# A two-layer recurrent and attention kernel on one core: loads of the first chunk on one queue, its copies on VectorE, B prepared early, and the norms of layer 0 in one ordered list

## The chip, the cores and the metric

The kernel runs on one core of a Trainium2 chip. The engines of the core are named as the profile names them: PE (TensorE, matrix products; PEld is its weight load), DVE (VectorE), ACT (ScalarE), POOL (GpSimd) and SP (SyncE, which here only issues loads and stores). Each works through its own queue in order and they meet at semaphores. The metric is device time in microseconds (us); the median of three runs is used, and one further execution is profiled. All times below are us unless another unit stands there.

## The reference

Input x is 16 sequences of 256 tokens of 256 numbers, f32, so 4096 tokens. Two layers follow, each of the form x + s * silu(g), with s and g computed from the same layer norm of x. Layer 0 has a complex diagonal recurrence for s and a GELU network for g; layer 1 has latent attention with 16 heads for s and a base matrix with a two-expert low-rank addition for g. Cut to layer 0, which the change touches:

```python
xn = _layernorm(x, axis=-1)
# s: recurrence with 32 complex states
A_re, A_im = mag * cos(theta), mag * sin(theta)     # mag = exp(-exp(softplus(nu_log)))
gamma = sqrt(clip(1.0 - mag * mag, 0.0))
Bu_re, Bu_im = xn @ (gamma * B_re).T, xn @ (gamma * B_im).T
new_re = A_re * h_re - A_im * h_im + bu_re          # scanned over the 256 tokens
new_im = A_re * h_im + A_im * h_re + bu_im
s = H_re @ C_re.T - H_im @ C_im.T + D * xn
# g: feed-forward
h = gelu(xn @ proj1.T + proj1_bias)                 # 256 -> 1024
g = silu(h @ proj2.T + proj2_bias)                  # 1024 -> 256
x = x + s * g
xn = _layernorm(x, axis=-1)                         # then layer 1 in the same form
```

## The kernel before, in words

The 4096 tokens are cut into 8 chunks of 512 tokens (two sequences each). A chunk lies in SBUF as four tiles of 128 tokens by 256 numbers and stays there through both layers. Layer 0 goes over all chunks, then layer 1 over all chunks; layer 1's code is not touched.

For a chunk of layer 0 these names matter:

- `layer_norm`, called by `norm0(ch)`: on DVE, statistics of four tiles (`bn_stats`, `bn_aggr`) and `ve` = variance + eps; on POOL a power, `rs`; on DVE again four subtract-and-multiply instructions that give `xn`.
- `turn0(ch, xn)`: PE transposes the eight 128 x 128 blocks of xn into PSUM (`tp`), and one copy by ACT and one by DVE give `xnT`.
- `hidden(ch, xnT)`: PE makes `ph` from `p1T` and xnT, ACT applies GELU, giving `hT`, eight blocks.
- `recur(ch, xnT)`: PE makes `pb` from `bT` (B, scaled and transposed) and xnT. DVE multiplies it by `turn`, a table of angles, giving `v`; two transfers over SP swap its halves into `w`; POOL adds; DVE scans with `decay` and multiplies again, giving `g`.
- `fold_heads(g)`, for chunks 0 to 3: small products (`psq`, `pso`) that fold weights of layer 1.
- `mix(ch, jp, hT)`: PE makes `pf` from hT and `p2T` for half a chunk; DVE adds a bias and ACT applies SiLU, giving `zf`.
- `finish0`: PE makes `py` from g and `csc` (C, signed); POOL and DVE put the new x together (`dx`).

The tables come from the two columns of `par`: exponents computed by polynomial (`exp_of`), `mag`, `gam`, the gain `gs`, the angle's sine and cosine (`sh`, `chf` on ACT), doublings of angle (`rot`), then `turn`, `decay`, `bsc` (B scaled) and `csc`. These are about 200 instructions on a few columns, most of them 0.15 to 0.25 on DVE.

What sets the order: instructions that are free are placed by a scheduler when the program is built, by its own estimate of when things are ready. Where a function calls an `InOrder` object instead of an engine, each instruction gets a dependency on the last one of that object, so their order on that engine is the written one. All of PE's work goes through one such object, `pe`. In layer 0 there are also `v0` for DVE, `a0` for ACT and `g0` for POOL. `Later` holds the small instructions of the tables back in a list and writes them out by count, so that they can be laid between other work. `start()` writes out chunk 0 by hand: two half chunks, with norm, transposes and hidden products, and table work between them.

Before the change, `v0` holds the work of `start()`, the table work and the norms of chunks 1 to 3. The norms of chunks 4 to 7, the products `v`, the copy of `bT`, and the powers in `layer_norm` are free for the scheduler. In the main loop the written order of a chunk from 2 on is: hidden, recur, (fold_heads), norm0 and turn0 of the next chunk, mix of the first half, finish0, mix of the second half, finish0. The same loop for chunks 0 and 1 is written a little differently, with the turn of B (`turn_b`) after the hidden products of chunk 1.

The loads: SP issues the four tiles of chunk 0 first (line 109), then half of p2T, the other chunks and layer 1's weights. ACT issues both halves of p1T (lines 224 and 225), the bias, signs, B, C, half of p2T and two broadcast rows (up to line 234). POOL issues par. All instructions that go through an `InOrder` object carry line 52 in the profile.

Of the kernel before, what the change touches and what calls it, by code (L numbers as in the profile page):

```python
# [11 lines left out]
F32 = mybir.dt.float32  # L12
I32 = mybir.dt.int32
AF = mybir.ActivationFunctionType
ALU = mybir.AluOpType
# [3 lines left out]
P = 128  # L19
B, S, D = 16, 256, 256  # L20
NTOK = B * S
CH = 512
NCH = NTOK // CH
TPC = CH // P
NST = 32
FF = 1024
# [14 lines left out]
def tile_two_layers(ctx: ExitStack, tc: tile.TileContext, d: dict, out: bass.AP):  # L41
    nc = tc.nc
# [23 lines left out]
    class Later:  # L66


        def __init__(self):
            self.todo = []  # L70

        def on(self, engine):
            later = self
# [7 lines left out]
            return Engine()  # L81

        def write(self, n=None):
            n = len(self.todo) if n is None else n
            for f in self.todo[:n]:
                f()
            del self.todo[:n]

    pe = InOrder(nc.tensor)

# [7 lines left out]
    X = []  # L98
# [1 line left out]
        xt = xpool.tile([P, TPC, D], F32, tag=f"x{ch}", name=f"x{ch}")  # L100
        X.append(xt)

    def load_x(ch):
        nc.sync.dma_start(
            X[ch], x_dram[ch * CH : (ch + 1) * CH, :].rearrange("(j p) e -> p j e", p=P)
        )

    for j in range(TPC):
        nc.sync.dma_start(X[0][:, j, :], x_dram[j * P : (j + 1) * P, :])

    ident = const.tile([P, P], F32, tag="ident", name="ident")
    make_identity(nc, ident)
# [46 lines left out]
        nc.sync.dma_start(desc, d["desc"])  # L159


    def layer_norm(pool, src, dst, tag, v=nc.vector):
        st = pool.tile([P, TPC, 6], F32, tag="ln_st", name=f"st_{tag}")
        mv = pool.tile([P, TPC, 2], F32, tag="ln_mv", name=f"mv_{tag}")
        ve = pool.tile([P, TPC], F32, tag="ln_ve", name=f"ve_{tag}")
        rs = pool.tile([P, TPC], F32, tag="ln_rs", name=f"rs_{tag}")
        for j in range(TPC):
            v.bn_stats(st[:, j, :], src[:, j, :])
        for j in range(TPC):
            v.bn_aggr(mv[:, j, :], st[:, j, :])  # L170
        v.tensor_scalar(ve, mv[:, :, 1], LN_EPS, None, ALU.add)
        nc.gpsimd.tensor_tensor(rs, ve, mhalf, ALU.pow)
        for j in range(TPC):
            v.tensor_scalar(
                dst[:, j, :], src[:, j, :], mv[:, j, 0:1], rs[:, j : j + 1],
                ALU.subtract, ALU.mult,
            )

    def transpose_rows(psum, ptag, src, dst, tag):
        for c in range(2):  # L180
            ps = psum.tile([P, CH], F32, tag=ptag, name=f"tp_{tag}_{c}")
            for j in range(TPC):
                pe.transpose(
                    ps[:, j * P : (j + 1) * P], src[:, j, c * P : (c + 1) * P], ident
                )
            if c == 0:
                nc.scalar.copy(dst[:, c, :], ps)
            else:
                nc.vector.tensor_copy(dst[:, c, :], ps)

    def bc(ap, n):

        return ap.unsqueeze(1).to_broadcast([ap.shape[0], n, ap.shape[1]])
# [6 lines left out]
    with ExitStack() as l0:  # L200
# [19 lines left out]

        p1d = d["proj1T"].rearrange("(c p) f -> p c f", p=P)
        p2d = d["proj2T"].rearrange("(c p) f -> p c f", p=P)
        nc.gpsimd.dma_start(par, d["par"])
        nc.scalar.dma_start(p1T[:, 0, :], p1d[:, 0, :])
        nc.scalar.dma_start(p1T[:, 1, :], p1d[:, 1, :])
        nc.scalar.dma_start(b1, d["proj1_b"])
        nc.scalar.dma_start(sgn, d["signs"])
        nc.scalar.dma_start(bst, d["B_stack"])
        for r in range(2):
            nc.scalar.dma_start(cst[64 * r : 64 * r + 64, :], d["C_stack"][r, 64 * r : 64 * r + 64, :])  # L230
        for z in range(2):
            (nc.sync, nc.scalar)[z].dma_start(p2T[:, 4 * z : 4 * z + 4, :], p2d[:, 4 * z : 4 * z + 4, :])
        nc.scalar.dma_start(b2_bc, d["proj2_b"].partition_broadcast(P))
        nc.scalar.dma_start(d_bc, d["D"].partition_broadcast(P))
        for ch in range(1, NCH):
            load_x(ch)
        load_layer1(wraw)

        def norm0(ch):
            xn = a2.tile([P, TPC, D], F32, tag="xn", name=f"xn0_{ch}")  # L240
            layer_norm(sm, X[ch], xn, f"0_{ch}", v0 if ch < 4 else nc.vector)
            return xn

        def turn0(ch, xn):
            xnT = a2.tile([P, 2, CH], F32, tag="xnT", name=f"xnT0_{ch}")
            transpose_rows(ps_mm, "mm", xn, xnT, f"0_{ch}")
            return xnT


        v0 = InOrder(nc.vector)  # L250
        a0 = InOrder(nc.scalar)
        later = Later()
        g0 = InOrder(nc.gpsimd)
        pv, pa, pg = later.on(v0), later.on(a0), later.on(g0)
# [30 lines left out]
        arg = tiny("arg")  # L285
        pv.tensor_scalar(arg, ex[:, 0:1], 1.0, -1.0, ALU.add, ALU.mult)
        mag = exp_of(arg, 1, "b")
        gam = tiny("gam")
        pv.tensor_tensor(gam, mag, mag, ALU.mult)
        pv.tensor_scalar(gam, gam, -1.0, 1.0, ALU.mult, ALU.add)  # L290
        pv.tensor_scalar(gam, gam, 0.0, None, ALU.max)
        gsq = tiny("gsq")
        pg.tensor_tensor(gsq, gam, phalf, ALU.pow)
        gs = tiny("gs")
        pv.tensor_tensor(gs, gsq, sgn[:, 0:1], ALU.mult)


        th = ex[:, 1:2]
        k2 = tiny("k2")
# [12 lines left out]
        pv.tensor_scalar(rr, rr, 3.2, -3.2, ALU.min, ALU.max)  # L312
        pv.tensor_scalar(ab, rr, -1.0, None, ALU.mult)
        pv.tensor_tensor(ab, ab, rr, ALU.max)
        pa.activation(sh, rr, AF.Sin, scale=0.5)
        pa.activation(chf, ab, AF.Sin, bias=halfpi, scale=-0.5)

        rot = w0.tile([P, 8, 2], F32, tag="rot", name="rot")
        u = tiny("u")
        f = tiny("f")  # L320
# [41 lines left out]
        pv.tensor_scalar(decay, decay, mag, None, ALU.mult)  # L362
        pv.memset(decay[:, :, 0:1], 0.0)

        bT = w0.tile([P, 2, P], F32, tag="bT", name="bT")
        bsc = w0.tile([P, D], F32, tag="bsc", name="bsc")
        pv.tensor_scalar(bsc, bst, gs, None, ALU.mult)

        def turn_b():
            psb = ps_mm.tile([P, 2, P], F32, tag="mm", name="psb")  # L370
            for c in range(2):
                pe.transpose(psb[:, c, :], bsc[:, c * P : (c + 1) * P], ident)
            nc.vector.tensor_copy(bT, psb)


        csc = w0.tile([P, D], F32, tag="csc", name="csc")
# [55 lines left out]
        def recur(ch, xnT):  # L432

            pb = ps_mm.tile([P, 2, S], F32, tag="mm", name=f"pb_{ch}")
            for c in range(2):
                pe.matmul(
                    pb.rearrange("p b s -> p (b s)"), bT[:, c, :], xnT[:, c, :],
                    start=(c == 0), stop=(c == 1),
                )
            v = a2.tile([P, 2, S], F32, tag="v", name=f"v_{ch}")  # L440
            nc.vector.tensor_tensor(v, pb, bc(turn, 2), ALU.mult)
# [39 lines left out]
        def start():  # L481
# [18 lines left out]
            def apply(js):  # L500
                for j in js:
                    v0.tensor_scalar(
                        xn[:, j, :], X0[:, j, :], mv[:, j, 0:1], rs[:, j : j + 1],
                        ALU.subtract, ALU.mult,
                    )
                z = slice(js[0] * P, (js[1] + 1) * P)
                ps = ps_mm.tile([P, 2, 2 * P], F32, tag="mm", name=f"tp_0_0_{js[0]}")
                for c in range(2):
                    for j2, j in enumerate(js):
                        pe.transpose(  # L510
                            ps[:, c, j2 * P : (j2 + 1) * P], xn[:, j, c * P : (c + 1) * P], ident
                        )
                a0.copy(xnT[:, :, z], ps)

            def hide(js, f0, f1):
                z = slice(js[0] * P, (js[1] + 1) * P)
# [7 lines left out]
                    a0.activation(hT[fc][:, z], ph, AF.Gelu, bias=b1[:, fc : fc + 1])  # L524

            stats((0, 1))
            later.write(7)
            apply((0, 1))
            stats((2, 3))
            later.write(8)  # L530
            hide((0, 1), 0, 4)
            apply((2, 3))
            hide((0, 1), 4, NFC)
            hide((2, 3), 0, NFC)
            later.write(30)
            xn2 = norm0(1)
            later.write()
            return xn, xnT, hT, xn2

        xn, xnT, hT, xn2 = start()  # L540
# [637 lines left out]
```

## Time and profile before

| what | us |
|---|---|
| median of three runs (973.28 to 975.37) | 975.35 |
| profiled execution | 976.5 |
| its span, first to last instruction | 974.7 |
| PE busy, 0 to 31 | 17.61 of 31 |
| PE busy, 31 to 64 | 28.84 of 33 |
| PE busy, 64 to 80 (granted clock 0.60) | 15.65 of 16 |
| PE busy, 80 to 184 | 104.00 of 104 |
| PE busy, 184 to 310 | 123.59 of 126 |
| PE busy, 310 to 930 | 614.22 of 620 |
| PE busy, 930 to 975 | 37.84 of 45 |

The lower part of the table is a cut of the span into stages: layer 0 ends a little before 300, and layer 1 fills the rest. The granted clock is the share of full speed that PE's throttle allowed; its mean over the span is 0.989. A PE that is busy at a granted clock of 0.5 takes about twice as long for the same products: chunk 0's `psq`, at 67.89, takes 3.51, and chunk 2's, at 113.39, takes 1.89. The busy share of the other engines is an average over stages with different limits and says nothing of what a change in one stage is worth. A row of the timeline gives start, duration, engine, line and operation, then output and inputs; neighbouring instructions of one kind are merged (x4), and a bracket at the end tells how long the engine had been idle and who released it.

### The profile page before, as it was taken

The page shows a single profiled execution, that of the slowest core. Times are in us where ns is not written, and L with a number is a line of the kernel's source. Part 1 is how long each engine was busy: PE and PEld are TensorE (multiplying, and loading weights), DVE is VectorE, ACT ScalarE, POOL GpSimd, SP SyncE. Part 2 cuts the span into 40 slices and gives each one's busy share as a digit, 9 for nine tenths or more (in the row PEclk, how much of TensorE's full clock was granted, in tenths as well). Part 3 has the DMA queues.
Part 4 walks back from the last instruction along what each step waited for, and adds up shares of the span by engine and source line. Part 5 has one row for each costly group of instructions (what it writes and reads, how often), then busy time and mean ns, then how long its engine had stood idle before and what let it go on. Part 6 is the DMA issues. An engine that isn't in the chain of part 4 may idle for free.

```text
span 974.7 us, 15632 instructions
## 1 busy us (share of the span) xinstructions
PE 941.8 (97%) x4730; PEld 678.9 (70%) x4730; DVE 597.2 (61%) x1880; ACT 429.0 (44%) x1422; POOL 421.0 (43%) x743
## 2 busy tenths in 40 slices
PE   4989999999999989999999999999999999999988
PEld 3848567666765656777777767777777777777776
DVE  5664414211215868967886796786688678677662
ACT  2321332233223545654564554555455455446540
POOL 3024333123313553554465445465545535536440
PEclk9979999999999999999999999999999999999999
DMA  9503000000001377787676778667767767777770
GB/s 307 179 14 116 12 1 11 11 11 1 11 12 23 93 191 202 192 214 177 182 194 197 170 179 211 168 178 202 193 162 190 213 173 185 192 182 189 219 198 28
DMA packets 197299, 136.04 MB, mean 140 GB/s; under 512 B 142432, under 2 KB 186848, under 8 KB 197216
## 3 DMA queue, kind: packets, MB, share of 16 engines
q1 hardware_dynamic: 194144, 129.27, 50.8%
q0 software_dynamic: 1376, 3.67, 1.0%
q10 hardware_dynamic: 1696, 2.10, 0.7%
q8 instruction: 38, 0.62, 0.3%
q14 instruction: 45, 0.37, 0.1%
HBM read 63.18 MB, written 52.95 MB: 119 GB/s over the span
## 4 chain that ended last, share of the span: by engine, by line
PE 87%; DVE 6%; DMA 2%; POOL 2%; issue 1%; SPq 1%; ACT 1%; ACTq 0%; POOLq 0%; DVEq 0%
PE pq L52 21%; PE sc L52 14%; PE po L52 10%; PE ph L52 10%; PE pf L52 9%; PE av L52 9%; PE pg L52 4%; PE pb L52 2%; PE pm L52 2%; PE py L52 1%; PE tp L52 1%; PE pkv L52 1%; PE psq L52 1%; SPq L52 1%; DMA x<-in_x_dram 1%
## 5 line engine op out<-in xcount | busy, mean ns | idle before, releaser
L52 ACT ACTIVATE pr<-sc,nm 128x256 f32<-128x256 f32 (+7 forms) x512 | 190.0, 381 | 285.8 <-DVE sr L52 193.6
L52 POOL TENSOR_SCALAR pr<-pr,sr 128x256 f32<-128x256 f32 (+7 forms) x512 | 192.3, 395 | 276.1 <-DVE sr L52 274.8
L52 PEld LDWEIGHTS sc<-kT,qg 128*128 128x128 f32 x1024 | 160.2, 191 | 63.4 <-issue 39.0
L52 PE MATMUL sc<-kT,qg 128*128 128x256 f32 (+7 forms) x1024 | 177.1, 307 | 5.6 <-DMA qg<-qrot 4.1
L52 DVE STREAM_TRANSPOSE turned<-pr 128x512 f32<-128x512 f32 x186 | 123.4, 688 | 14.8 <-POOL pr L52 14.0
L52 DVE TENSOR_REDUCE nm<-sc 128x1 f32<-128x256 f32 (+7 forms) x512 | 127.7, 301 | 6.6
L52 PE MATMUL pq<-xnT,wlat 128*128 128x512 f32 x256 | 123.7, 607 | 0.0
L52 PE MATMUL pq<-xnT,wrope 128*128 128x512 f32 x256 | 120.1, 593 | 0.0
L52 PE MATMUL ph<-xnT,p1T 128*128 128x512 f32 (+1 forms) x288 | 113.6, 554 | 4.4 <-ACT xnT L52 4.4
L52 PE MATMUL po<-wout,attT 128*128 128x256 f32 x512 | 115.8, 380 | 0.0
L52 PE MATMUL pf<-p2T,hT 128*128 128x256 f32 x512 | 113.1, 379 | 0.0
L52 PEld LDWEIGHTS po<-wout,attT 128*128 128x128 f32 x512 | 96.4, 190 | 20.9 <-issue 6.4
L52 PEld LDWEIGHTS pf<-p2T,hT 128*128 128x128 f32 x512 | 96.7, 190 | 13.7 <-issue 0.9
L52 ACT ACTIVATION_READ_ACCUMULATOR pr<-sc,nm 128x1 f32 x512 | 103.5, 202 | 0.0
L52 PEld LDWEIGHTS ph<-xnT,p1T 128*128 128x128 f32 x288 | 56.0, 195 | 57.6 <-issue 49.5
L52 PE MATMUL av<-pT,row 128*64 128x256 f32 (+1 forms) x1024 | 90.5, 329 | 0.2 <-DMA pT<-far 0.2
L52 POOL TENSOR_TENSOR qrot<-qmul,qmul 128x512 f32<-128x512 f32 x64 | 83.0, 1317 | 14.2 <-DVE sc L52 9.8
L52 DVE TENSOR_TENSOR qmul<-pq,rot_q 128x512 f32<-128x512 f32 x128 | 80.9, 675 | 0.0
L52 PEld LDWEIGHTS av<-pT,row 128*64 128x64 f32 x1024 | 64.2, 137 | 22.9 <-issue 0.5
L52 ACT ACTIVATE qg<-pq 64x512 f32<-64x512 f32 x128 | 75.5, 590 | 6.1 <-PE pq L52 5.4
L52 DVE TENSOR_TENSOR sc<-sc,kmask 128x96 f32<-128x96 f32 (+1 forms) x192 | 46.1, 240 | 50.2 <-PE sc L52 48.9
L52 PEld LDWEIGHTS pq<-xnT,wlat 128*128 128x128 f32 x256 | 46.2, 193 | 32.2 <-issue 32.1
(164 smaller groups left out, 912.7 us busy)
## 6 DMA issues: line engine op xcount, KB each, us to landing
far<-turned SPq DMA_DIRECT2D x248, 192.0 KB, 3.7
pT<-far SPq DMA_DIRECT2D x62, 768.0 KB, 4.8
qg<-qrot SPq DMA_DIRECT2D x256, 64.0 KB, 2.3
x<-in_x_dram SPq DMA_DIRECT2D x7, 512.0 KB, 8.9
out_dram<-o POOLq DMA_DIRECT2D x28, 128.0 KB, 3.4
wqn<-in_wq_nopeT_dram SPq DMA_DIRECT2D x4, 512.0 KB, 4.9
wo<-in_Wo_dram SPq DMA_DIRECT2D x4, 512.0 KB, 5.8
w<-v SPq DMA_DIRECT2D x16, 128.0 KB, 2.3
```

Of the source, the lines that this page charges most:

```text
L52: r = getattr(self.engine, name)(*args, **kw)
```

## The change

It has four parts.

1. Loads of chunk 0. All of them but four go to SP, in a written order: the four x tiles, the second half of p1T (now cut by columns of the hidden layer), B, chunk 1, p2T, two broadcast rows, C. ACT issues par, the first half of p1T, the bias and the signs.
2. Copies. In `start()`, the copies of the transposes of chunk 0 go from ACT to DVE, in v0's order; chunk 1's go through a0 and v0. The table work is laid out anew: marks in the `Later` list replace counts, the angle comes before the gain, and chunk 1's transposes move into `start()`.
3. B. `bsc` is computed at the end of the gain, not after the tables; its turn on PE moves between the two mixes of chunk 0, and its copy moves from DVE to ACT in a0's order.
4. Norms. `norm0` uses v0 and g0 for every chunk, and `v` in `recur` goes through v0 as well.

```diff
-    for j in range(TPC):
-        nc.sync.dma_start(X[0][:, j, :], x_dram[j * P : (j + 1) * P, :])
...
-    def layer_norm(pool, src, dst, tag, v=nc.vector):
+    def layer_norm(pool, src, dst, tag, v=nc.vector, g=nc.gpsimd, between=None):
...
-        nc.gpsimd.tensor_tensor(rs, ve, mhalf, ALU.pow)
+        g.tensor_tensor(rs, ve, mhalf, ALU.pow)
+        if between:
+            between()
...
-        nc.gpsimd.dma_start(par, d["par"])
-        nc.scalar.dma_start(p1T[:, 0, :], p1d[:, 0, :])
-        nc.scalar.dma_start(p1T[:, 1, :], p1d[:, 1, :])
-        nc.scalar.dma_start(b1, d["proj1_b"])
-        nc.scalar.dma_start(sgn, d["signs"])
-        nc.scalar.dma_start(bst, d["B_stack"])
+        s0 = InOrder(nc.sync)
+        a0 = InOrder(nc.scalar)
+        a0.dma_start(par, d["par"])
+        for j in range(TPC):
+            s0.dma_start(X[0][:, j, :], x_dram[j * P : (j + 1) * P, :])
+        for z, e in ((0, a0), (1, s0)):
+            fz = slice(z * FF // 2, (z + 1) * FF // 2)
+            e.dma_start(p1T[:, :, fz], p1d[:, :, fz])
+        a0.dma_start(b1, d["proj1_b"])
+        a0.dma_start(sgn, d["signs"])
+        s0.dma_start(bst, d["B_stack"])
+        load_x(1, s0)
+        for z in range(2):
+            s0.dma_start(p2T[:, 4 * z : 4 * z + 4, :], p2d[:, 4 * z : 4 * z + 4, :])
+        s0.dma_start(b2_bc, d["proj2_b"].partition_broadcast(P))
+        s0.dma_start(d_bc, d["D"].partition_broadcast(P))
         for r in range(2):
-            nc.scalar.dma_start(cst[64 * r : 64 * r + 64, :], d["C_stack"][r, 64 * r : 64 * r + 64, :])
-        for z in range(2):
-            (nc.sync, nc.scalar)[z].dma_start(p2T[:, 4 * z : 4 * z + 4, :], p2d[:, 4 * z : 4 * z + 4, :])
-        nc.scalar.dma_start(b2_bc, d["proj2_b"].partition_broadcast(P))
-        nc.scalar.dma_start(d_bc, d["D"].partition_broadcast(P))
-        for ch in range(1, NCH):
+            s0.dma_start(cst[64 * r : 64 * r + 64, :], d["C_stack"][r, 64 * r : 64 * r + 64, :])
+        for ch in range(2, NCH):
             load_x(ch)
...
-        def norm0(ch):
+        def norm0(ch, between=None):
             xn = a2.tile([P, TPC, D], F32, tag="xn", name=f"xn0_{ch}")
-            layer_norm(sm, X[ch], xn, f"0_{ch}", v0 if ch < 4 else nc.vector)
+            layer_norm(sm, X[ch], xn, f"0_{ch}", v0, g0, between)
...
-            transpose_rows(ps_mm, "mm", xn, xnT, f"0_{ch}")
+            if ch == 1:
+                transpose_rows(ps_mm, "mm", xn, xnT, f"0_{ch}", a0, v0)
+            else:
+                transpose_rows(ps_mm, "mm", xn, xnT, f"0_{ch}")
...
-            nc.vector.tensor_copy(bT, psb)
+            a0.copy(bT, psb)
...
-            nc.vector.tensor_tensor(v, pb, bc(turn, 2), ALU.mult)
+            v0.tensor_tensor(v, pb, bc(turn, 2), ALU.mult)
...
-                a0.copy(xnT[:, :, z], ps)
+                return ps
+
+            def keep(js, ps):
+                v0.tensor_copy(xnT[:, :, js[0] * P : (js[1] + 1) * P], ps)
...
             stats((0, 1))
-            later.write(7)
+            later.write(4)
             apply((0, 1))
+            ps = turn((0, 1))
             stats((2, 3))
-            later.write(8)
+            keep((0, 1), ps)
+            later.write(3)
+            apply((2, 3))
             hide((0, 1), 0, 4)
-            apply((2, 3))
+            ps = turn((2, 3))
+            later.write("exp")
+            keep((2, 3), ps)
             hide((0, 1), 4, NFC)
             hide((2, 3), 0, NFC)
-            later.write(30)
-            xn2 = norm0(1)
+            xn2 = norm0(1, lambda: later.write("angle"))
+            later.write("gain")
+            xnT2 = turn0(1, xn2)
             later.write()
...
             if ch == 0:
 
-                xnT2 = turn0(1, xn2)
-                zf = [mix(ch, jp, hT) for jp in range(2)]
+                zf = [mix(ch, 0, hT)]
+                turn_b()
+                zf.append(mix(ch, 1, hT))
                 hT = hidden(1, xnT2)
-                turn_b()
                 g = recur(ch, xnT)
```

More of the change, by code (lines that the diff above doesn't have):

```diff
@@ L69, in __init__, with mark @@
         def __init__(self):
-            self.todo = []
+            self.todo, self.done, self.marks = [], 0, {}
+        def mark(self, name):
+            self.marks[name] = self.done + len(self.todo)
         def on(self, engine):
@@ L83, in write @@
         def write(self, n=None):
+            if isinstance(n, str):
+                n = self.marks[n] - self.done
             n = len(self.todo) if n is None else n
@@ L87, in write @@
             del self.todo[:n]
+            self.done += n
     pe = InOrder(nc.tensor)
@@ L101, in tile_two_layers, with load_x @@
         X.append(xt)
-    def load_x(ch):
-        nc.sync.dma_start(
+    def load_x(ch, e=nc.sync):
+        e.dma_start(
             X[ch], x_dram[ch * CH : (ch + 1) * CH, :].rearrange("(j p) e -> p j e", p=P)
         )
-    for j in range(TPC):
-        nc.sync.dma_start(X[0][:, j, :], x_dram[j * P : (j + 1) * P, :])
     ident = const.tile([P, P], F32, tag="ident", name="ident")
@@ L177, in layer_norm, with transpose_rows @@
             )
-    def transpose_rows(psum, ptag, src, dst, tag):
+    def transpose_rows(psum, ptag, src, dst, tag, a=nc.scalar, v=nc.vector):
         for c in range(2):
@@ L186, in transpose_rows @@
             if c == 0:
-                nc.scalar.copy(dst[:, c, :], ps)
+                a.copy(dst[:, c, :], ps)
             else:
-                nc.vector.tensor_copy(dst[:, c, :], ps)
+                v.tensor_copy(dst[:, c, :], ps)
     def bc(ap, n):
@@ L245, in turn0 @@
             xnT = a2.tile([P, 2, CH], F32, tag="xnT", name=f"xnT0_{ch}")
-            transpose_rows(ps_mm, "mm", xn, xnT, f"0_{ch}")
+            if ch == 1:
+                transpose_rows(ps_mm, "mm", xn, xnT, f"0_{ch}", a0, v0)
+            else:
+                transpose_rows(ps_mm, "mm", xn, xnT, f"0_{ch}")
             return xnT
         v0 = InOrder(nc.vector)
-        a0 = InOrder(nc.scalar)
         later = Later()
@@ L283, in tile_two_layers @@
         ex = exp_of(par, 2, "a")
[L285 to L295, printed above, removed]
+        later.mark("exp")
         th = ex[:, 1:2]
@@ L314, in tile_two_layers @@
         pv.tensor_tensor(ab, ab, rr, ALU.max)
+        later.mark("angle")
         pa.activation(sh, rr, AF.Sin, scale=0.5)
         pa.activation(chf, ab, AF.Sin, bias=halfpi, scale=-0.5)
+        arg = tiny("arg")
+        pv.tensor_scalar(arg, ex[:, 0:1], 1.0, -1.0, ALU.add, ALU.mult)
+        mag = exp_of(arg, 1, "b")
+        gam = tiny("gam")
+        pv.tensor_tensor(gam, mag, mag, ALU.mult)
+        pv.tensor_scalar(gam, gam, -1.0, 1.0, ALU.mult, ALU.add)
+        pv.tensor_scalar(gam, gam, 0.0, None, ALU.max)
+        gsq = tiny("gsq")
+        pg.tensor_tensor(gsq, gam, phalf, ALU.pow)
+        gs = tiny("gs")
+        pv.tensor_tensor(gs, gsq, sgn[:, 0:1], ALU.mult)
+        bT = w0.tile([P, 2, P], F32, tag="bT", name="bT")
+        bsc = w0.tile([P, D], F32, tag="bsc", name="bsc")
+        pv.tensor_scalar(bsc, bst, gs, None, ALU.mult)
+        later.mark("gain")
         rot = w0.tile([P, 8, 2], F32, tag="rot", name="rot")
@@ L363, in tile_two_layers @@
         pv.memset(decay[:, :, 0:1], 0.0)
-        bT = w0.tile([P, 2, P], F32, tag="bT", name="bT")
-        bsc = w0.tile([P, D], F32, tag="bsc", name="bsc")
-        pv.tensor_scalar(bsc, bst, gs, None, ALU.mult)
         def turn_b():
@@ L505, in apply, with turn @@
                     )
-                z = slice(js[0] * P, (js[1] + 1) * P)
+            def turn(js):
                 ps = ps_mm.tile([P, 2, 2 * P], F32, tag="mm", name=f"tp_0_0_{js[0]}")
@@ L526, in start @@
             stats((0, 1))
-            later.write(7)
+            later.write(4)
             apply((0, 1))
+            ps = turn((0, 1))
             stats((2, 3))
-            later.write(8)
+            keep((0, 1), ps)
+            later.write(3)
+            apply((2, 3))
             hide((0, 1), 0, 4)
-            apply((2, 3))
+            ps = turn((2, 3))
+            later.write("exp")
+            keep((2, 3), ps)
             hide((0, 1), 4, NFC)
             hide((2, 3), 0, NFC)
-            later.write(30)
-            xn2 = norm0(1)
+            xn2 = norm0(1, lambda: later.write("angle"))
+            later.write("gain")
+            xnT2 = turn0(1, xn2)
             later.write()
-            return xn, xnT, hT, xn2
-        xn, xnT, hT, xn2 = start()
+            return xn, xnT, hT, xn2, xnT2
+        xn, xnT, hT, xn2, xnT2 = start()
         for ch in range(NCH):
```

## The prediction

> **What bounds the kernel now.** All times are us. I read the page first, then the chain that ended last (87% of it PE), then the timeline of layer 0 and the windows view for the clock. The row of PE says that this is a kernel of one busy engine, so a change pays only where PE stands still or is clocked down.
>
> ```profile
> span 974.7 us, 15632 instructions
> PE 941.8 (97%) x4730; PEld 678.9 (70%) x4730; DVE 597.2 (61%) x1880; ACT 429.0 (44%) x1422; POOL 421.0 (43%) x743
> PEclk9979999999999999999999999999999999999999
> ```
>
> Three places in layer 0 stand out when the timeline is cut to PE. The first is the start (columns: start, duration, engine, line, operation; in brackets the idle time before and what ended it):
>
> ```profile
> 8.95 1.22 PE L52 MATMUL tp<-ident,xn 128*128 128x128 f32 x4 [8.95 <-DVE xn L52]
> 12.16 0.49 ACTq L234 DMA_DIRECT2D d_bc<-in_D_dram  x1
> 12.68 1.28 ACT L52 ACT_TABLE_LOAD   x1 [12.68 <-DMA cst<-in_C_stack_dram]
> 13.97 0.59 ACT L52 COPY xnT<-tp 128x512 f32<-128x512 f32 x1
> 14.61 5.79 PE L52 MATMUL ph<-xnT,p1T 128*128 128x256 f32 x16 [4.44 <-ACT xnT L52]
> ```
>
> The transposes of the first half chunk are done at 10.17, but their copy to SBUF stands in ACT's queue behind ten loads, the last of which is issued at 12.65, and behind a table load of 1.28. PE waits 4.44. The second place is B:
>
> ```profile
> 59.46 0.38 PE L52 MATMUL psb<-ident,bsc 128*128 128x128 f32 x2
> 64.35 3.75 PE L52 MATMUL pb<-xnT,bT 128*128 128x512 f32 x4 [4.51 <-DVE bT L373]
> 67.89 3.51 PE L52 MATMUL psq<-wkb,wqn 128*128 128x64 f32 x16
> ```
>
> B is turned at 59.5 and used at once; its copy bT waits in DVE's queue behind the norm statistics of chunks 4 to 7, and PE idles 4.51. The windows view shows the granted clock fall to 0.50 at about 63.3 and come back at 76.8, so what follows runs at half speed. The third place is well now, and is what I weigh most: chunk 4 on PE, with DVE beside it.
>
> ```profile
> 181.19 1.88 PE L52 MATMUL pb<-xnT,bT 128*128 128x512 f32 x4
> 182.91 1.04 PE L52 MATMUL tp<-ident,xn 128*128 128x128 f32 x8
> 183.78 2.54 PE L52 MATMUL pf<-p2T,hT 128*128 128x256 f32 x11
> ...
> 172.48 1.38 DVE L174 TENSOR_SCALAR xn<-x,mv,rs 128x256 f32<-128x256 f32 x4 [4.13 <-POOL dx L476]
> 183.11 0.69 DVE L441 TENSOR_TENSOR v<-pb,turn 128x512 f32<-128x512 f32 x1 [9.25 <-PE pb L52]
> ```
>
> PE goes from pb (input of the recurrence, chunk 4) straight into tp (transposes of chunk 5's norm) because DVE wrote that norm, xn, at 172.5, some 9 us before v, which waits for pb.
>
> **The start.** Six of ACT's loads move to SP, and ACT keeps par, half of p1T, b1 and sgn. The copy of the transposes goes to DVE, in its order behind the statistics of rows 2 and 3. Take the second x tile as landed at 6.07, as now: two statistics, aggregates and ve end at 6.92, POOL's power at 7.79. Only 4 small exponent instructions (0.19 each) stand before the subtract, not 7, and par no longer comes through POOL (issued there at 1.36, landed at 7.16); so the subtract begins at 7.85 instead of 8.48, its two end at 8.58, the transposes at 9.54. Statistics of rows 2 and 3 take 1.38 (9.13 to 10.50 now), to 10.0; then the copy, 0.69 by the DVE row of the same size: 10.69. The first hidden matmul starts at 10.74 instead of 14.61: **3.9 saved**. x tile 3 has landed by 9.69 in this trace (its statistics start without a wait), and half a p1T less now competes with it; the other half of p1T, sent in the slot where p2T landed at about 9.6, is needed at about 16. If the x tiles come 0.5 earlier 4.4 is saved; if par or x comes 1.5 later, 2.4.
>
> The Trainium skill's "DMA: Bandwidth & Descriptors" (section "Issuing engines are not separate DMA queues") says that spreading issues over engines saves only the sequencer's issue time, usually little. By that rule the moved issues are worth their own time, 0.34 + 1.17 + 0.39 + 0.35 + 0.49 = 2.7. The rows say more: between them ACT's queue waited for earlier loads to land, so it was shut from 0.73 to 12.65. I follow the rows, and the sum above does not rest on the issue time, since DVE is late next.
>
> **What follows in chunk 0.** From 10.74 the hidden matmuls run as before (16.7 from first to last, the slow first four included), to 27.4. The second copy waits on DVE for its transposes at about 17, then chunk 1's statistics, power, subtract (4.4 by the rows at 53.58 to 57.97, plus nine angle instructions, 1.6, of which 1 lies beside POOL's power) end near 23: 4 before PE asks. The gain chain (22 instructions, 4.0; power and two products 1.3) ends near 28 with bsc; its turn on PE is at 35. Cost nothing; without this cover (POOL stuck behind the wrope copies, whose load lands at 28.05) PE would lose up to 5. The rest of the small work, 33.26 to 53.58 now, ends near 49.5, before pb at 56.
>
> **B.** Its turn moves between the two mixes and its copy to ACT, 20 us ahead of use: the 4.51 wait goes, and with it the slow clock. The span from pb of chunk 0 to the first pf of chunk 1 is 79.69 - 64.35 = 15.34; at full clock pb, psq and pso take 116.22 - 111.67 = 4.55 per chunk, twice 9.10. **Saved: 4.5 + 6.2 = 10.7.** All gains: 14.6.
>
> **Norms in written order.** v now goes into the same ordered DVE list as every norm. The program writes recur(ch), with v, ahead of norm0(ch+1), and turn0(ch+1) behind that, ahead of mix. So for chunks 2 to 6 the norm of the next chunk can only start when v is done, v waits for pb, and PE's own order puts tp right behind pb. What hid the norm, 9 us of lead, is gone. Price, from the end of pb: v 0.04 + 0.69 + 0.03; statistics to last subtract 4.39 (rows below, POOL's power inside); the last four transposes and pf behind them 0.64. Together 5.79, against 183.78 - 183.07 = 0.71 now:
>
> ```profile
> 53.58 1.41 DVE L52 BATCH_NORM_STATS2 st<-x 128x6 f32<-128x256 f32 x4
> 54.91 0.36 DVE L52 BATCH_NORM_AGGREGATE mv<-st 128x2 f32<-128x6 f32 x4
> ...
> 56.59 1.38 DVE L52 TENSOR_SCALAR xn<-x,mv,rs 128x256 f32<-128x256 f32 x4 [1.12 <-POOL rs L172]
> ```
>
> **5.1 lost in each of chunks 4, 5 and 6: 15.2.** In chunks 2 and 3, psq and pso stand between pb and tp (pf comes 3.60 after pb's end at 146.43 + 1.88), so 2.2 each: 4.4, or 2.9 each if the copy of psq (0.69) gets in between. In chunk 1 the first pf and py (8.7) cover it: nothing. POOL's sum of v and w, 1.26, starts 3.75 after pb's end (117.30), just as the power would end (2.73 to 3.74); if it goes first, 2.3 more per chunk.
>
> **The clock in the new gaps.** Each gap holds 4.2 of pure idle, then sparse transposes. The rows: after 59.84 the clock fell 3.4 into the idle, and stayed low for 13, costing 6.2. After a sparse stretch near 938 it fell in an idle of 1.85, and was back about 3 later (a row of the timeline, and one of the windows view, whose last three columns are granted clock, DMA share and GB/s):
>
> ```profile
> 940.67 1.54 PE L52 MATMUL pt<-ident,pr 128*128 128x128 f32 x6 [1.85 <-POOL pr L52]
> 941.00:942.00 1.00, 1.00 (x6) 1.00 (x5) 0.00 (x0) 0.18 (x1) 0.83 (x3) 0.50 0.99 284
> ```
>
> The Trainium skill's "TensorE: Matmul & The Clock Gate" (Part 1) has the clock halved after a whole idle window of 3.4, free-running, and restored after a busy one. An idle of 4.2 contains a whole window with a chance of (4.2 - 3.4)/3.4 = 0.24, and each fall then costs half of 3.4: as an estimate 0.4 per gap, 1.2 in all. By the rows a fall is likely, and dense matmuls at half speed (as the 16 at 14.61, 5.79 instead of 3.5) cost 2 or so. I take 0.85 x 2 = 1.7 for each of three gaps and 0.7 for the two short ones: 6.5. Bounds: 0, and 3 x 6.2 by the row of chunk 0.
>
> **Sum.** 15.2 + 4.4 + 6.5 = 26.1 lost, 14.6 gained: 11.5 slower. The profiled execution took 976.5 (span 974.7 and 1.8 around it), 1.15 above the median of 975.35; so 988.0 beside it, and 986.9 against the median. I say **986.5**.
>
> **Rivals.**
> - *The norm stays hidden*: DVE still has xn ready before pb. For it: the lead of 9 us in the trace. Against it: v and the norm share one list, and DVE in the trace idles at v for 9.25 rather than pass it. Then only gains remain: 975.35 - 14.6 = 960.7. It decides at one point: whether the statistics of chunk ch+1 start before v of chunk ch.
> - *The clock stays low and POOL is in the way*: each long gap costs 5.1 + 6.2 + 2.3, the short ones 4.5: 40.8 + 9 - 14.6 = 35, so 1010. For it, the 13 us of slow clock after 63.3; against it, that stretch held narrow psq and pso matmuls, where here dense pf follow.
> - *The gaps cost less*: without a fall of the clock (26.1 - 6.5 = 19.6 lost) and with 4.4 gained at the start it is +4.5, so 980, the forecast's own low end. No change needs 4.5 more: the subtracts (1.38) and last transposes beside pf in each of three gaps, which PE's order forbids, or a cheaper start. Near 976.
>
> **Numbers.** The forecast, gaps with some clock loss, 0.80; norm hidden 0.07; slow clock and POOL 0.08; little or no difference 0.05. Its own bounds: +4.5 (no fall of the clock, 4.4 at the start), with 0.8 for the unknown of the first tiles' landing, and +21 (the bound of the clock in two of three gaps, 2 x 4.5 more than I took), so 979 to 996. The other cases lie outside it, 2 in 10. A change under 0.3% (2.9) can't be told from none here. Chances: faster 0.07, same 0.05, slower 0.88.
>
> **What will show it.** Right: first ph near 10.7; pb of chunk 0 near 56 with no wait for bT; PE idle about 4 before tp in chunks 4 to 6, ended by xn of DVE, with v just before the statistics; the clock row below 9 in slices 4 to 10. Wrong: tp following pb at once in those chunks, statistics ahead of v, or a first ph later than 13.

## The result, and the profile after

The changed kernel takes 998.17 (median of 5 runs, 997.49 to 999.44) against 975.35 before: a ratio of 1.0241, with a 95% interval of 1.0225 to 1.0256. It is 22.8 slower, where 11.5 was forecast, and lies above the forecast's range of 979 to 996. Its profiled execution took 999.44, with a span of 997.7. The page after, its first rows (for the changed kernel: span, PE's busy time, PE's busy tenths and its clock in 40 slices of 25 us):

```profile
span 997.7 us, 15633 instructions
PE 949.8 (95%) x4730; PEld 683.9 (69%) x4730; DVE 602.1 (60%) x1881; ACT 426.4 (43%) x1420; POOL 419.9 (42%) x742
...
PE   7999889789799989999999999999999999999988
PEclk9999889899899999999999999999999999999999
```

PE's busy time is up by only 8.0, the span by 23.0: most of the loss is PE standing still, and where it stands still the clock row has an 8. The 8s lie in slices 4 to 10, counted from 0, about 100 to 275. From the timeline, PE in the changed kernel, first the start and B:

```profile
6.50 1.23 PE L52 MATMUL tp<-ident,xn 128*128 128x128 f32 x4 [6.50 <-DVE xn L52]
8.69 6.77 PE L52 MATMUL ph<-xnT,p1T 128*128 128x256 f32 x16 [0.97 <-DVE xnT L52]
33.88 0.38 PE L52 MATMUL psb<-ident,bsc 128*128 128x128 f32 x2
...
55.45 1.88 PE L52 MATMUL pb<-xnT,bT 128*128 128x512 f32 x4
```

The first hidden product comes 5.9 earlier than before, and pb of chunk 0 follows without a wait, at full clock (1.88, where it took 3.75). When the first pf of chunk 1 begins, at 64.67 against 79.69, the changed kernel is 15.0 ahead. Then chunk 4, first on PE and after the dots on DVE and POOL:

```profile
179.41 1.88 PE L52 MATMUL pb<-xnT,bT 128*128 128x512 f32 x4
186.55 2.21 PE L52 MATMUL tp<-ident,xn 128*128 128x128 f32 x8 [5.26 <-DVE xn L52]
188.56 8.97 PE L52 MATMUL pf<-p2T,hT 128*128 128x256 f32 x32
...
181.33 0.69 DVE L52 TENSOR_TENSOR v<-pb,turn 128x512 f32<-128x512 f32 x1 [14.76 <-PE pb L52]
181.93 1.39 DVE L52 BATCH_NORM_STATS2 st<-x 128x6 f32<-128x256 f32 x4
184.94 2.44 DVE L52 TENSOR_SCALAR xn<-x,mv,rs 128x256 f32<-128x256 f32 x4 [1.12 <-POOL rs L52]
...
183.89 1.01 POOL L52 TENSOR_TENSOR rs<-ve,mhalf 128x4 f32<-128x4 f32 x1 [13.22 <-DVE ve L52]
185.00 1.26 POOL L462 TENSOR_TENSOR v<-v,w 128x512 f32<-128x512 f32 x1
```

DVE stands at v for 14.76 with the whole norm of chunk 5 behind it, though that norm's input has long been there. PE, done with pb, waits 5.26 for xn. Then tp takes 2.21, where it took 1.04, and pf 8.97, where it took 7.07. The windows view of the same chunk (third column from the end: granted clock) has PE at half speed there, and back at full speed near the end of pf:

```profile
189.00:190.00 1.00, 1.00 (x4) 0.82 (x3) 1.00 (x2) 0.00 (x0) 0.00 (x0) 0.50 0.00 0
...
193.00:194.00 1.00, 1.00 (x6) 0.87 (x6) 0.00 (x0) 0.00 (x0) 0.00 (x0) 1.00 0.00 0
```

The gaps of all five chunks, from the end of pb to the start of pf, with the time of the first pf behind each, give the ledger of layer 0 (each from PE's timeline):

| | chunk 2 | chunk 3 | chunk 4 | chunk 5 | chunk 6 | sum |
|---|---|---|---|---|---|---|
| gap before | 3.60 | 3.60 | 0.71 | 0.71 | 0.71 | 9.3 |
| gap after | 8.55 | 8.89 | 7.27 | 7.30 | 7.16 | 39.2 |
| pf before | 7.07 | 7.07 | 7.07 | 7.07 | 7.07 | 35.4 |
| pf after | 8.70 | 8.34 | 8.97 | 7.58 | 8.64 | 42.2 |

That is 29.8 in the gaps and 6.9 in pf: 36.7 lost, against 15.0 gained, so 21.7; layer 1's first products (pkv) start 21.65 later than before (318.73 against 297.08). The last 1.3 of the span come in layer 1, whose code and order on PE are the same. From pkv to the end it took 677.6 before, 679.0 after, and between 677.4 and 681.1 in the experiments below; this scatter was not followed up.

### The profile page after: what moved, and what is told of

Same layout as the page of the kernel before. It is cut to its first block, busy times and chain, and to the rows that moved or that the text cites. A ratio compares the mean times of both kernels' runs of the same rounds, so it can differ in the third digit from the quotient of the medians.

```text
span 997.7 us, 15633 instructions
## 1 busy us (share of the span) xinstructions
PE 949.8 (95%) x4730; PEld 683.9 (69%) x4730; DVE 602.1 (60%) x1881; ACT 426.4 (43%) x1420; POOL 419.9 (42%) x742
## 4 chain that ended last, share of the span: by engine, by line
PE 77%; DVE 8%; POOL 5%; issue 5%; DMA 3%; SPq 2%; ACT 1%; POOLq 0%; ACTq 0%
PE pq L52 19%; PE sc L52 13%; PE po L52 10%; PE pf L52 8%; PE av L52 8%; PE ph L52 7%; PE pg L52 4%; SPq L52 2%; PE tp L52 2%; PE pm L52 1%; DVE xn L52 1%; PE pkv L52 1%; POOL pr L52 1%; DMA qg<-qrot 1%; DMA pT<-far 1%
## 5 line engine op out<-in xcount | busy, mean ns | idle before, releaser
L52 PE MATMUL pf<-p2T,hT 128*128 128x256 f32 x512 | 120.1, 395 | 0.0
L52 PEld LDWEIGHTS pf<-p2T,hT 128*128 128x128 f32 x512 | 102.0, 201 | 15.6 <-issue 0.9
```

The source lines that it names most:

```text
L52: r = getattr(self.engine, name)(*args, **kw)
```

## Experiments

Three questions were open: whether the place of the norm behind v is the whole loss; what each part is worth alone; and why the gaps cost 36.7 where 26.1 were forecast. The experiments fall into three groups, each with its own runs of the kernel before; their medians are 974.05, 972.65 and 975.72, so each time comes with its ratio to the kernel before.

**The norm's place.** One word of the change is undone:

```diff
-            v0.tensor_tensor(v, pb, bc(turn, 2), ALU.mult)
+            nc.vector.tensor_tensor(v, pb, bc(turn, 2), ALU.mult)
```

> The changed kernel with one word undone: v of the recurrence is free again, the norms stay in v0's order. Theory A (the norm waits in DVE's list behind v, and all of the loss hangs on that): the five gaps before tp in chunks 2 to 6 are gone, 36.7 us of the ledger come back, about 961 us, below the kernel before by the 15 us of start and B. Rival B (the norms' order itself, g0's powers or DVE's load in layer 0 is what costs): most of the loss stays, above 985 us.

It took 962.19, ratio 0.9873 (0.9839 to 0.9906). All five gaps are as before (3.60 and 0.71), and pf takes 7.07. PE and DVE of chunk 4 in this kernel:

```profile
167.07 1.88 PE L52 MATMUL pb<-xnT,bT 128*128 128x512 f32 x4
168.79 1.04 PE L52 MATMUL tp<-ident,xn 128*128 128x128 f32 x8
...
158.37 1.38 DVE L52 TENSOR_SCALAR xn<-x,mv,rs 128x256 f32<-128x256 f32 x4 [4.14 <-POOL dx L492]
159.66 1.40 DVE L52 BATCH_NORM_STATS2 st<-x 128x6 f32<-128x256 f32 x4
```

xn is ready 9 ahead of the end of pb, and even the next chunk's statistics have gone ahead of v. The norms are still in one ordered list here, so the list itself costs nothing. The other way to lift the block leaves v in the list and writes the norm before it:

```diff
             else:
+                if 1 < ch < NCH - 1:
+                    xn2 = norm0(ch + 1)
                 g = recur(ch, xnT)
...
                 if ch + 1 < NCH:
-                    xn2 = norm0(ch + 1)
+                    if ch == 1:
+                        xn2 = norm0(ch + 1)
```

> The changed kernel with v still in v0, but the norm of the next chunk written ahead of recur from chunk 2 on, so that it stands ahead of v in the list. Theory A: it is the place in the list, not membership, so again about 961 us, with xn ready before pb. Rival B (a single ordered list for DVE is too stiff wherever the norm stands): 975 us or more.

964.37, ratio 0.9893 (0.9853 to 0.9932), gaps as before: it is the order inside the list. The two ratios' intervals overlap, but the runs stand in one group and do not (961.83 to 963.15, then 964.10 to 965.01), so the first way is about 2 faster. Part of it shows in the trace: in chunks 4 and 5 of the second kernel PE waits 0.79 each before py, for g, which the first kernel does not.

**The parts alone.** Each is put on the kernel before. First, the norms' part (cut: `layer_norm` also takes the engine for its power):

```diff
-            layer_norm(sm, X[ch], xn, f"0_{ch}", v0 if ch < 4 else nc.vector)
+            layer_norm(sm, X[ch], xn, f"0_{ch}", v0, g0)
...
-            nc.vector.tensor_tensor(v, pb, bc(turn, 2), ALU.mult)
+            v0.tensor_tensor(v, pb, bc(turn, 2), ALU.mult)
```

> The kernel before with only the fourth part of the change: norms on v0 and g0, v in v0; loads, copies and B as before. Theory A: 36 us of gaps come in; since the norms of chunks 2 to 7 can no longer stand ahead of bT's copy, the 4.5 us wait for bT and its 6.2 us of slow clock go, so 975.35 + 36 - 10 = 1001 us. Rival C (the gaps come from chunk 0 and the new start, or from turn0's place): no gaps in chunks 2 to 6, 965 to 976 us.

1002.87, ratio 1.0291 (1.0254 to 1.0328). The gaps are there without any of the other parts: 8.55, 8.89, 7.28, 7.29 and 7.28, with 42.0 in the five pf. And pb of chunk 0 starts at 60.82, after a wait of 0.61 for ACT: with the norms behind v, nothing stands ahead of bT's copy any more. So this part also brings the gain of B; the two are not to be added. Next, B:

```diff
-            nc.vector.tensor_copy(bT, psb)
+            a0.copy(bT, psb)
...
-                zf = [mix(ch, jp, hT) for jp in range(2)]
-                hT = hidden(1, xnT2)
+                zf = [mix(ch, 0, hT)]
                 turn_b()
+                zf.append(mix(ch, 1, hT))
+                hT = hidden(1, xnT2)
```

(bsc is also written right after gs.)

> The kernel before with only the third part: bsc right after the gain, its turn between the mixes, its copy on ACT in a0's order. Theory A: the 4.5 us wait and 6.2 us of slow clock go, nothing else moves: 964.6 us. Rival: the slow clock after 63.3 has another cause, then only 4.5 us: 970.9 us.

966.29, ratio 0.9917 (0.9891 to 0.9942): 8 less, not 10.7. In the trace pb of chunk 0 starts at 60.10 with no wait and at full clock, and the first pf of chunk 1 at 69.32, 10.4 earlier than in the kernel before: as far as there the sum holds. Then PE waits where it had not waited, in chunk 1 for the sum dx on DVE and in chunk 2 for GELU on ACT:

```profile
80.44 1.13 PE L52 MATMUL py<-csc,g 128*128 128x256 f32 x4 [1.35 <-DVE dx L476]
...
96.88 7.13 PE L52 MATMUL ph<-xnT,p1T 128*128 128x512 f32 x16 [0.67 <-ACT hT L427]
```

Layer 1 starts only 7.8 earlier (289.25). So "nothing else moves" does not hold for B alone; in the changed kernel PE has neither wait. The time is also compared with more than one execution: the 10.7 was read from one whose mean clock was 0.989. The 17 runs of the kernel before in the second group spread from 970.02 to 976.65: all seven from 970.02 to 971.72 have a mean clock of 0.995, all seven above 974 have 0.989 to 0.993. It may be that the slow clock behind the wait for bT is shorter in the faster ones; no profile of one shows it. In the next kernel the work behind a wait of 5.20 was slow for about 4, against 12 in the profile of the kernel before.

The start alone is the change without B's and the norms' edits:

> The kernel before with only parts one and two: loads, copies and table order; B and the norms as before. Theory A: first hidden product at 8.7 us instead of 14.6, of which about 5 stay behind the slow clock of the start; the wait for bT stays, so 970 us. Rival: the earlier start runs into the wait for bT, which only grows, because DVE's table work and hoisted statistics set when bT is copied; then little is left, 974 us.

968.52, ratio 0.9952 (0.9936 to 0.9968). The first hidden product comes at 9.03. The wait for bT stays, a little longer:

```profile
53.99 0.38 PE L52 MATMUL psb<-ident,bsc 128*128 128x128 f32 x2
59.57 3.75 PE L52 MATMUL pb<-xnT,bT 128*128 128x512 f32 x4 [5.20 <-DVE bT L390]
63.11 2.15 PE L52 MATMUL psq<-wkb,wqn 128*128 128x64 f32 x16
```

Start and B together: 0.9952 x 0.9917 = 0.987, within the interval of the first experiment.

**The size of the gaps: the clock.** PE is kept at work in the gaps by products whose result nothing reads:

```diff
                     xn2 = norm0(ch + 1)
+                    if ch > 1:
+                        pz = ps_y.tile([P, 2, D], F32, tag="py", name=f"pz_{ch}")
+                        for _ in range(4 if ch < NH // HG else 5):
+                            pe.matmul(pz.rearrange("p b s -> p (b s)"), bT[:, 0, :], xnT[:, 0, :], start=True, stop=True)
```

> The changed kernel with work added to PE that nothing reads: 4 products (chunks 2, 3) or 5 (chunks 4 to 6) of bT and xnT between pb and tp, 0.86 us each, shorter than the gaps of 3.8 to 5.3 us. Theory A, with a clock that falls for idleness: tp takes 1.0 instead of 2.2 us (of which 0.65 is on the path, since xn sets the pace) and pf 7.07 instead of 7.6 to 9.0, about 2.0 us in each of five chunks, 988 us. Rival D (the clock follows something else, or the slow pf is not the clock): no change, or slower by the added work, 998 us or more.

989.68, ratio 1.0183 (1.0147 to 1.022). PE has 23 products more to do (46 matmuls in the trace, two for each), about 0.9 each, and the kernel is faster: all five pf take 7.07 (6.9 less than after), and each gap is about 0.5 shorter (2.6 in all), because tp runs at full clock. Chunk 4, from PE's timeline and the windows view of 170 to 190:

```profile
175.91 4.45 PE L52 MATMUL pz<-xnT,bT 128*128 128x512 f32 x10
181.35 1.65 PE L52 MATMUL tp<-ident,xn 128*128 128x128 f32 x8 [0.98 <-DVE xn L52]
...
170.00:190.00 20.00, 19.02 (x67) 11.61 (x66) 7.33 (x17) 2.65 (x4) 2.28 (x2) 1.00 0.06 14
```

In the changed kernel the same view of 176 to 196 gives 0.83. By the ledger the clock's fall in the gaps was worth 9.5: 6.9 in pf and 2.6 in tp. The medians differ by 8.5, the ratios by 0.0058 or 5.7, so its size in time is less sure than its place.

**POOL's sum.** In chunks 2 to 6 it is taken from POOL and put on DVE behind the norm, which is handed to `recur` (cut):

```diff
-            nc.gpsimd.tensor_tensor(v, v, w, ALU.add)
+            if norm:
+                norm()
+                v0.tensor_tensor(v, v, w, ALU.add)
+            else:
+                nc.gpsimd.tensor_tensor(v, v, w, ALU.add)
```

> The changed kernel with the sum of v and w taken from POOL and put on DVE behind the subtracts of the next norm, in chunks 2 to 6. Theory E (the first subtract of xn is held until POOL's sum has ended[...]): the four subtracts take 1.38 instead of 2.3 to 2.5 us and tp starts 1.0 us earlier in each of five chunks, 993 us. Rival (xn is slow for another reason, such as its inputs): subtracts as before, 998 us, or more for the sum's 0.7 us on DVE.

987.79, ratio 1.0166 (1.0133 to 1.0199). Chunk 4 on DVE and PE:

```profile
177.80 1.38 DVE L52 TENSOR_SCALAR xn<-x,mv,rs 128x256 f32<-128x256 f32 x4 [1.12 <-POOL rs L52]
...
178.36 2.21 PE L52 MATMUL tp<-ident,xn 128*128 128x128 f32 x8 [4.21 <-DVE xn L52]
```

The four subtracts take 1.38 again, and the gaps of chunks 4, 5 and 6 are 6.21, 6.23 and 6.21: shorter by 1.06, 1.07 and 0.95. In chunk 4 of the changed kernel POOL's sum runs from 185.00 to 186.26, the chain of waits shows the first subtract of xn busy from 184.94 for 1.48, and tp is released just then: the subtract lasts as long as the sum runs. In chunk 6 the sum starts 0.57 after the subtracts, and there PE's second wait for xn (0.80) is what goes. In chunks 2 and 3 the gaps shrink by more, 1.9 and 2.8: the scheduler now puts wlat behind the aggregates as well, and in chunk 3 the clock stays up; there the effects are mixed.

**wlat.** This is the copy of psq that the scheduler, not the written order, puts between the statistics of chunks 2 and 3. Chunk 2 of the changed kernel:

```profile
100.41 0.69 DVE L422 COPY wlat<-psq 128x512 f32<-128x512 f32 x1 [0.70 <-PE psq L52]
```

It goes to ACT in both:

```diff
-            nc.vector.tensor_copy(
+            (nc.scalar.copy if g > 1 else nc.vector.tensor_copy)(
                 wlat[:, :, hs, :], psq.rearrange("p c a b f -> p c (a b) f")
```

> The changed kernel with the copy of psq (wlat) on ACT instead of DVE in chunks 2 and 3. Theory: that copy stands between the statistics in DVE's queue and waits there for psq, 0.7 us of idleness and 0.6 of its own, so tp comes 1.3 us earlier in each of the two chunks: 995.6 us. Rival (the gap of chunks 2 and 3 is that of the clock and POOL alone): 998 us.

998.54 (995.52 to 1000.47), ratio 1.0271 (1.0234 to 1.0309): no gain in time. The trace has one: in the changed kernel DVE does one of the four statistics, idles 0.70 for psq, copies wlat for 0.69 and only then goes on; here the four run through, and the gaps are 7.16 and 7.91, shorter by 1.4 and 1.0. But the five pf behind the gaps took 43.9 in this execution, 1.7 more than after, and layer 1 took 1.2 more. The four runs follow the mean clock, 995.52 at 0.984 and 1000.47 at 0.979. The time alone neither supports nor refutes the expectation.

**All three together.** wlat on ACT, the sum on DVE, and the unread products (1 in chunks 2 and 3, 4 in the others):

> The changed kernel with its three unforeseen terms taken out together: the sum of v and w on DVE behind the norm, wlat on ACT in chunks 2 and 3, and unread products on PE (1 in chunks 2 and 3, 4 in chunks 4 to 6) that keep the clock up. Theory A: what is left is the sum of the prediction without its clock term: pf starts 5.8 us after pb's end in all five chunks and takes 7.07, 19.6 lost against 15 gained, 980 us. Rival (something else also waits): 984 us or more, with gaps above 6.2 us.

982.84, ratio 1.0076 (1.0059 to 1.0094). The gaps are 5.70, 6.45, 5.68, 5.69 and 5.68, and pf takes 7.07 in each: 19.9 lost, where the prediction's sum has 19.6 without the clock (15.2 and 4.4). Chunk 3's 0.7 is layer 1's first norm, two of whose statistics the scheduler puts between those of chunk 4. The profiled execution is at 300.96 when layer 1 starts, 3.9 after the kernel before; the other 3.5 of its span come in layer 1, within the scatter named above.

**The start.** The first hidden product came 2.0 earlier than forecast. The statistics that it waits for last are those of the second x tile; they began at 4.27, where 6.07 was carried over. The first tile's began at 2.88, not 4.92. Two edits of the loads, both on the first experiment's kernel (there 2.87, 4.97, and the product at 9.39), ask about the first tile:

```diff
-            fz = slice(z * FF // 2, (z + 1) * FF // 2)
-            e.dma_start(p1T[:, :, fz], p1d[:, :, fz])
+            e.dma_start(p1T[:, z, :], p1d[:, z, :])
```

> e1 with p1T cut as it was before, by rows of 4 KB (c = 0 on ACT, c = 1 on SP), not by columns into 2 KB pieces. Theory F (the first x tile lands at 2.9 instead of 4.9 us because p1T's pieces that compete with it are half as long): first statistics at 4.5 to 5 us. Rival G (it is the order: par ahead of p1T on ACT, one p1T load less in front): first statistics at 2.9 us as in e1.

First statistics at 2.88: the cut of p1T does not matter for it (964.27, ratio 0.9885, 0.9871 to 0.99).

```diff
-        a0.dma_start(par, d["par"])
...
+        a0.dma_start(par, d["par"])
         a0.dma_start(b1, d["proj1_b"])
```

> e1 with par behind p1T's half on ACT, so that p1T starts at 0.7 us as in the kernel before. Theory G (par ahead of p1T gives the first x tile 0.4 us of free engines): first statistics at 4 to 5 us, and the first hidden product 1 to 2 us later than in e1. Theory F (length of pieces): first statistics near 3 us, hidden product as in e1.

First statistics at 3.56 (965.05, ratio 0.989, 0.9875 to 0.9904): p1T's half ahead of par on ACT's queue delays the first tile by 0.7; the other 1.3 may come from the second p1T load on ACT, which was not tried by itself. The second tile's statistics began at 5.26 and the first hidden product at 9.69, not the 1 to 2 later that was expected: with the new loads unchanged they range from 4.27 to 5.07 and from 8.69 to 9.49 over the kernels here. Last, an attempt to use the time before 6.5, with ten products of ident put first on PE, unread:

> e1 (v free) with ten products of ident and ident put on PE ahead of the first transposes, read by nobody, while PE waits for the first norm. Theory A: the first 16 hidden products take 3.5 us instead of 5.7, since the clock is up when they come: 960 us, below every kernel so far. Rival: the start's clock does not depend on PE's own work before, or the added work delays the transposes: 962 us or more.

963.98, ratio 0.9876 (0.9856 to 0.9896), no gain over the first experiment. The first sixteen matmuls of the hidden layer still take 6.33, against 5.30 to 6.77 without the added work:

```profile
1.48 4.64 PE L52 MATMUL pz<-ident 128*128 128x128 f32 x20 [1.48 <-POOL ident masks.py:199]
6.64 1.23 PE L52 MATMUL tp<-ident,xn 128*128 128x128 f32 x4 [0.52 <-DVE xn L52]
8.83 6.33 PE L52 MATMUL ph<-xnT,p1T 128*128 128x256 f32 x16 [0.97 <-DVE xnT L52]
```

So PE had been at work for 5.9 of the 7.3 before, with narrow matmuls, and the start's slowness stays. The profile's clock column reads 1.00 here in all kernels, so it does not show what slows them; this stays open.

The first experiment's kernel, 962.19, is the lowest of all, 1.3% below the kernel before; those with other loads or the added work at the start are not told apart from it by their ratios.

## Why the prediction was right and wrong

**Right: the mechanism, its place and its sign.** The norm behind v in DVE's list, five gaps before tp, with chunk 1 spared, and a clock that falls in them: one word undone removes all of it. The rival in which the norm stays hidden named the deciding point, statistics ahead of v, and gave 960.7 for a kernel without the gaps; the first experiment, which is such a kernel, took 962.19. The gains, 14.6 in the sum, were 15.0 in the trace, in part by luck: see the start below.

**Wrong: the size of the loss, 36.7 for 26.1.** The step that failed is the price of a gap, in three terms of the sum.

- *The subtracts, 1.38 inside the 4.39 for a norm.* They took 2.3 to 2.5. The row of 1.38 came from a place where POOL was idle. I did set POOL's sum beside POOL's power, and saw that the sum starts just as the power ends; I asked only which of the two goes first on POOL, not what the sum does to DVE. It cost 1.06, 1.07 and 0.95 in chunks 4 to 6; in chunks 2 and 3, where no run isolates it, 0.95 each is left when the other terms are taken off. The Trainium skill's "SBUF — State Buffer" (section "Who interferes with whom") says that DVE and GpSimd share a pair of ports as an exclusive lock, so that a copy or scalar instruction of DVE in a two-port mode is fully blocked by a GpSimd instruction that began first. The runs agree in that the subtract ends with the sum, and is quick without it. They do not show who began first: in chunk 4 the subtract's row starts 0.06 ahead of the sum's (184.94 and 185.00). That the ports are the cause is the page's account; the runs show only that the sum on POOL is. By that rule, as an estimate, the sum of 1.26 would have put up to 1.3 more in each gap.
- *The two short gaps, 2.2 each.* They cost 5.0 and 5.3. The copy of wlat was named, at 0.69, as an upper case; it cost 1.4 in chunk 2 and 1.0 in chunk 3, since DVE also idles at it until psq is done. In chunk 3 two statistics of layer 1's norm came in too, 0.7. The rest is the hold above and tp's slow clock. Copy and statistics are the same thing as the change's own fault: on an engine that works in order, an instruction placed early waits with all that is behind it. I priced what the written order puts in DVE's list, not what the scheduler puts between.
- *The clock, 6.5.* It cost 9.5, by the run that keeps PE at work. Of this 6.9 is pf, near what was taken, and 2.6 is tp at half speed inside the gaps, which I had left out. All five gaps brought a fall, where 0.85 was put on the long ones and less on the short ones. That pf comes so near is in part luck: the row it was sized by, the sixteen matmuls of 5.79 at the start, has a granted clock of 1.00 in the windows view, so it is no case of a halved clock. The rule of the Trainium skill's "TensorE: Matmul & The Clock Gate" (Part 1) that the prediction cites, weighed at 1.2, is further off: it gave one fall in about four gaps.

Together: 5.8 more in the short gaps (10.2 for 4.4), 4.4 more in the long ones (19.6 for 15.2), tp's slow clock among both, and 0.4 more in pf: 10.6. The forecast's range took only the clock and the first tiles' landing as unknown, so neither POOL's hold nor wlat was in it. The run with these terms taken out comes to 19.9, so the rest of the working, v, statistics, power, subtracts and transposes at 5.79, holds to 0.1 in four chunks of five.

**The start** was mis-sized in two terms that cancelled in part. The first product came at 8.69, not 10.74, as the second x tile landed earlier; I had kept the old landing as given, though the loads around it were what changed. (Seven loads left ACT, not six, and par came from POOL; neither enters the sum.) But at pb of chunk 0 only 0.5 of that 2.0 is left (55.45 for 56): the first sixteen matmuls took 6.77 where 5.79 was carried over, and PE waited 0.45 for ACT between the hidden products of chunk 1. **B**'s 10.7 holds against the profiled execution up to chunk 1 (10.4 for B alone). B alone then lost 2.5 to waits that the rest of the change takes away, and its ratio says 8. The 10.7 also included 13 us of slow clock, which the faster runs of the kernel before, by their mean clock, may have less of; that is not shown. A sum made against one execution inherits that execution's clock.

## What to carry to other kernels

When an instruction enters an ordered list, look at what it waits for and then at everything written behind it in that list: independent work with a long lead loses the whole lead, 9 us in chunk 4 here. Write such work ahead of the waiting instruction, or leave the waiting one out of the list. When pricing the new gap, take durations from rows with the same neighbours: which engine works beside it at that moment, what the scheduler can slip in between, and at which clock the work behind the gap will run.

## What the runs showed of the hardware

- An idle time of PE of 3.8 to 5.3 before tp brought the clock to 0.50 in all five gaps of the changed kernel, and the dense products behind it took 0.5 to 1.9 more; which of these it is changes from gap to gap and run to run. The length alone does not decide: in the kernel with POOL's sum on DVE the clock fell after an idle time of 1.92 in chunk 2 (tp 2.21), and stayed up after one of 1.91 in chunk 3 (tp 1.64). Filling the gaps with unread products was quicker than leaving them empty: 9.5 less in layer 0's ledger, and a ratio of 1.0183 for 1.0241.
- A subtract on DVE that took 0.40 elsewhere lasted up to 1.5 while POOL's sum of 1.26 ran, and the set of four 2.3 to 2.5 instead of 1.38.
- Work on PE does not always make what follows quick: 20 narrow matmuls over 4.64 left the next wide ones as slow as without them (6.33 for sixteen, at a granted clock that reads 1.00).
- The first 128 KB tile landed 2.0 earlier (2.88 for 4.92) with the new loads, among which one load of 512 KB less, and a load of 1 KB more, stood at the head of ACT's queue; with the 1 KB behind the 512 KB it was 0.7 later (3.56).
